# Attention's small products in one run, and their sums moved ahead of the main products

## The chip, the cores and the metric

One core of a Trainium2 chip runs the whole program. The metric is the device time of the program in microseconds; the median of three runs is given, and one further execution was recorded by the profiler.

## The reference

The input x has 4 sequences of 512 times, 128 features and 64 channels (a time holds D = 8192 numbers). Layer 0 is an attention-like recurrence, a convolution over features, a convolution over time and a feed-forward net; layer 1 is a Fourier filter with a moving average. All is fp32. Cut to what matters here:

```python
xn = layernorm(x.reshape(b, t, d), ln_attn_g, ln_attn_b)
k, v, r = xn @ Wk, xn @ Wv, sigmoid(xn @ Wr)          # 64 wide
s = decay * s + k[t] * v[t]                           # over t
x = x + ((r * states) @ Wo).reshape(b, t, f, h)       # 64 -> 8192
xn = layernorm(x.reshape(b, t, d), ln_freq_g, ln_freq_b)
x = x + gelu(conv3_over_f(xn, freq_W) + freq_b)       # mixes the 64 channels
xn = layernorm(x.reshape(b, t, d), ...)               # then causal taps over t,
x = x + layernorm(taps3_over_t(xn))                   # channel by channel
x = x + gelu(x @ ffn_W1 + ffn_b1) @ ffn_W2 + ffn_b2
# layer 1
trend = moving_average(x, 25)
x = trend + irfft(einsum(rfft(x - trend)[:128], w_real + 1j * w_imag))
```

## The kernel before

A tile holds one chunk of D on the 128 partitions and 512 times along the free dimension; two chunks are worked on together, so a stage over one sequence has NPR = 32 steps. Layer 0's stages over a sequence b are generators: `project` (J: the products with Wk, Wv, Wr), `scan` (Z: the recurrence), `attend_and_convolve` (A: the changed one), `convolve_time` (C), `open_feed` (O) and `feed_forward` (F). The function `in_turn` runs two lists of stages side by side, each stage yielding shares of its work, and takes the list that is behind; so A0 (A of sequence 0) runs beside J1, A1 beside C0, A2 beside C1, A3 beside C2. TensorE's order is exactly the order in which the source issues its instructions (`manual_schedule`). On all other engines and on the DMA queues a scheduler orders the instructions.

A step of A works on one pair i of chunks:

- `attend(i)` loads the input pair xp and the weights wo_sb on SP's queue, multiplies the gated state rst with wo_sb into the one PSUM pair a (line 529: two products of 64 rows by 128 columns), adds xp on VectorE into x1 (531) and scales it by the row rb into z (535).
- `convolve(i - 2)` fills a PSUM pair cv. cv is tile c for odd pairs and tile m for even ones, but always c while J1 keeps its own result in m (`held`). Line 550 starts cv with four products that have two rows each: the rows are the convolution's image of the layer norm's scale and bias (`cgr`, loaded once from the DRAM tile `cgd`), times the row mb and a row of ones. Line 559 adds the neighbouring chunks (64x64 products), line 564 the chunks themselves (128x128, "main"). ScalarE applies gelu in place (565), VectorE adds x1 into x2 (567), POOL's queue stores x2 to DRAM (568), ScalarE squares it (570).
- `add_up(i - 3)` adds up x2 and its square over partitions, by products with ones of 32 columns, into the bank st (line 252; convolve_time's own sums go to bank p by the same line).

`x1`, `xp` and `wo_sb` have three buffers, `x2` and its square two. When the sums over all pairs are done, `finish` and `rows` make the mean and the scale of the next layer norm from them and spread them as rows for the next stage. The first stage, `project(0)`, runs alone: for each pair it loads weights, input pair xp and a slab xk in [time, D] order; the weights are multiplied with each other (399), scaled in place on VectorE (358) and used (409), while `statistics` (341) takes mean and variance of the slab on VectorE.

Every fp32 product is two instructions on TensorE, so "x4" in a row is two products.

Of the kernel before, what the change touches and what calls it, by code (L numbers as in the profile page):

```python
# [16 lines left out]
P = 128  # L17
T = 512
NF = 128
H = 64  # L20
# [60 lines left out]
def layer0(ctx, tc, dram, x, xt, vecs, wkvr, wo, wdec, wconv, fbias, w1, fb1, w2, fb2, x4):  # L81
# [67 lines left out]

    cgr = const.tile([P, NPR, H], F32, name="cgr")  # L150

# [17 lines left out]
    def prepare():  # L169
# [35 lines left out]
        for k in range(2):  # L205
            nc.scalar.dma_start(cgd[:, k, :], cgt[k * NCH : (k + 1) * NCH, :])
        cg4 = cgd.rearrange("(i j) k (h m) -> h j k i m", j=2, h=2)
        for h in range(2):
            for j in range(2):
                q = 32 * (2 * h + j)  # L210
                nc.scalar.dma_start(cgr[q : q + 2, :, :], cg4[h, j])

# [112 lines left out]
    def project(b):  # L325
# [41 lines left out]
        for i in range(NPR):  # L367
            first, last = i == 0, i == NPR - 1
            if b > 1:


                xks[i] = token_major(i, two(bk, "sq" if i % 2 else "x2"))
                if i % 2 == 0:
                    weights(i + 2)
                if not last:
                    xps[i + 1] = load_x(b, i + 1)
                wq, xp = ws.pop(i), xps.pop(i)
                for k in (i - 2, NPR - 2, NPR - 1) if last else (i - 2,):
                    if k in xks:
                        statistics(k, xks.pop(k))  # L380
            else:
                if unscanned[0]:

                    wq, xk = two(fr, "x1")[:, :, 0 : 4 * S + 3], spare("z", SL)
                else:

                    both = spare("wx", 4 * S + SL)
                    wq, xk = both[:, :, 0 : 4 * S], both[:, :, 4 * S :]
                n = 4 * S + 2 * (b == 0)
                nc.sync.dma_start(wq[:, :, 0 : n], wkvr[2 * i : 2 * i + 2, :, 0 : n].rearrange("c p s -> p c s"))  # L390
                xp = load_x(b, i)
                statistics(i, token_major(i, xk))
            if b == 0:
# [9 lines left out]
            if b < 2:  # L403
                scale_weights(i, wq)
            elif not last:
                scale_weights(i + 1, ws[i + 1], True)
# [108 lines left out]
    def attend_and_convolve(b):  # L515
# [3 lines left out]
        nc.vector.tensor_scalar(mb, mb, at_one[:, 1:2], at_one[:, 0:1], ALU.mult, ALU.add)  # L519
        x1s, zs, ws, waiting = {}, {}, {}, {}  # L520

        def attend(i):
            xp = load_x(b, i)
            wo_sb = fr.tile([P, P], F32, tag="wo", name="wo_sb")
            nc.sync.dma_start(wo_sb, wo[:, i, :])
            at = two(ps_a, "a")
            for j in range(2):
                js = slice(j * S, (j + 1) * S)
                nc.tensor.matmul(at[:, j, :], lhsT=wo_sb[js, :], rhs=rst[js, :], start=True, stop=True)  # L529
            x1 = x1s[i] = fr.tile([P, 2, SL], F32, tag="x1", name="x1")  # L530
            nc.vector.tensor_tensor(x1, at, xp, ALU.add)  # L531
            z = fr.tile([P, 2, SL], F32, tag="z", name="z", bufs=4)
            for j in range(2):
                zs[2 * i + j] = z[:, j, :]
            nc.vector.tensor_tensor(z, x1, pair_of(rb), ALU.mult)

        def scaled(i):

            wcs = fr.tile([P, 2, P + H], F32, tag="wcs", name="wcs")
            for j in range(2):  # L540
# [3 lines left out]

        def convolve(i):
            cv = c_bank() if i % 2 or held[0] else two(ps_m, "m")
            for h in range(2):
                for j in range(2):
                    q = 32 * (2 * h + j)
                    nc.tensor.matmul(  # L550
                        cv[h * H : (h + 1) * H, j, :], lhsT=cgr[q : q + 2, i, :], rhs=mb[q : q + 2, :],
                        start=True, stop=False,
                    )
            for j in range(2):
                c = 2 * i + j
                for n, h in neighbours(i % 2, c):
                    if 0 <= n < NCH:
                        rs = halves[rows_of(n // 2 % 2, n - c)]
                        nc.tensor.matmul(
                            cv[halves[h], j, :], lhsT=ws[n][rs, P:], rhs=zs[n][rs, :], start=False, stop=False  # L560
                        )
            for j in range(2):
                c = 2 * i + j
                nc.tensor.matmul(cv[:, j, :], lhsT=ws[c][:, 0:P], rhs=zs[c], start=False, stop=True)
            nc.scalar.activation(cv, cv, AF.Gelu_apprx_tanh)
            x2 = two(bk, "x2")
            nc.vector.tensor_tensor(x2, cv, x1s.pop(i), ALU.add)  # L567
            nc.gpsimd.dma_start(x2d[b][2 * i : 2 * i + 2].rearrange("c p t -> p c t"), x2)
            sq2 = bk.tile([P, 2, SL], F32, tag="sq", name="sq2")
            nc.scalar.activation(sq2, x2, AF.Square)  # L570
# [6 lines left out]

        for i in range(NPR + 3):

            while begin[attend_and_convolve] < b + (min(i, 3) - 3) / 4:  # L580
                yield BLOCKED
            if i < 2:
                scaled(i)
            if i < NPR:
                attend(i)
                yield 1.0
            if 1 < i < NPR + 2:
# [7 lines left out]
            if i > 2:  # L595
                add_up(st, i - 3, *waiting.pop(i - 3), i == 3, i == NPR + 2)
                yield 1.0
            if b == 0 and i >= NPR and i < NPR + 2:
# [598 lines left out]
```

## Time and profile before

| | us |
|---|---|
| median of 3 runs (3730.09 to 3739.56) | 3737.65 |
| the profiled execution | 3734.79 |
| its span, first to last instruction | 3733.0 |
| TensorE (PE) busy in it | 3521.2 |
| VectorE (DVE) busy in it | 2671.9 |
| ScalarE (ACT) busy in it | 1778.0 |

PE is TensorE's matmuls, PEld its weight loads (which overlap), DVE VectorE, ACT ScalarE, POOL GpSimd, SP the engine that issues most loads. Where a stretch is asked for, a row gives its bounds, its length, and the busy time of each engine with the number of instructions. In a listing in order of time, the columns are start, length, engine, line, operation, output and inputs, and in brackets the idle time before it with what ended it. Matmul ends are modelled, so the distances of starts say more than lengths. The attentions lie at these times: A0 from 220 to 475 us, A1 from 475 to 802, A2 from 1217 to 1463, A3 from 1873 to 2121; J0 fills 0 to 156, layer 1 everything from 2750 on.

### The profile page before, as it was taken

The numbers are of one execution on the slowest core, as the hardware profiler recorded it, in microseconds if no ns is written. First come the engines' busy times: TensorE is split into PE (matmuls) and PEld (weight loads), VectorE is DVE, ScalarE is ACT, GpSimd is POOL, SyncE is SP. The second block draws the span as 40 slices with busy tenths as digits, with TensorE's granted clock in tenths as the row PEclk, the third lists the DMA queues.
The fourth block names the chain that finished last, engine by engine and source line by source line (L and its number), as shares of the span: only waits on it lengthen the run. The fifth ranks groups of instructions, "written<-read, shape, count | busy, mean of one in ns | idle before, by whom it ended". The sixth has DMA issues, their size and how long they took to land. (4 is left out here: it accounts for less than half of the span.)

```text
span 3733.0 us, 53000 instructions
## 1 busy us (share of the span) xinstructions
PE 3521.2 (94%) x20041; PEld 1360.6 (36%) x20041; DVE 2671.9 (72%) x3498; ACT 1778.0 (48%) x2331; POOL 447.3 (12%) x654
## 2 busy tenths in 40 slices
PE   9999999999998999999989989999989999989998
PEld 4433322234333223433322233333323843328533
DVE  4455569976776896676789699946658277792677
ACT  0012346655656565565656578868854200152100
POOL 0000012210101221001122122100000000001000
PEclk9999999999999999999999999999999999999999
DMA  9867657787874687788578677645569478894687
GB/s 314 279 211 242 227 177 262 260 276 265 290 262 168 235 280 271 266 292 278 182 238 286 213 247 267 234 149 196 198 203 287 150 240 290 290 297 164 213 294 260
DMA packets 427223, 910.29 MB, mean 244 GB/s; under 512 B 32728, under 2 KB 83160, under 8 KB 422872
## 3 DMA queue, kind: packets, MB, share of 16 engines
q1 hardware_dynamic: 353136, 636.92, 52.5%
q0 software_dynamic: 71680, 268.46, 19.7%
q8 instruction: 160, 2.62, 0.3%
q10 hardware_dynamic: 2152, 1.51, 0.1%
q14 instruction: 95, 0.78, 0.1%
HBM read 638.26 MB, written 268.50 MB: 243 GB/s over the span
## 5 line engine op out<-in xcount | busy, mean ns | idle before, releaser
L745 PE MATMUL p<-mid,w_sb 64*64 64x512 f32 x2048 | 554.5, 599 | 20.3 <-DVE wx L758 20.3
L745 PE MATMUL pb<-mid,w_sb 64*64 64x512 f32 x2048 | 536.2, 598 | 0.0
L737 ACT ACTIVATE mid<-c,fb_sb 128x1024 f32<-128x1024 f32 x256 | 284.3, 1111 | 97.2 <-PE c L732 94.8
L737 ACT ACTIVATE mid<-m,fb_sb 128x1024 f32<-128x1024 f32 x256 | 284.6, 1112 | 93.5 <-PE m L732 92.1
L732 PE MATMUL c<-x,w_sb 64*64 64x512 f32 x2016 | 281.2, 611 | 13.2 <-ACT mid L737 6.9
L732 PE MATMUL m<-x,w_sb 64*64 64x512 f32 x2016 | 283.0, 612 | 6.7 <-ACT ob L777 4.9
L745 PEld LDWEIGHTS p<-mid,w_sb 64*64 64x64 f32 x2048 | 155.5, 135 | 294.9 <-issue 262.0
L409 PE MATMUL a<-xp,wx 128*128 128x512 f32 x512 | 242.6, 617 | 9.1 <-DVE wx L358 8.6
L1043 ACT COPY two<-a 128x512 f32<-128x512 f32 x64 | 37.5, 585 | 428.9 <-PE a L1038 428.9
L1066 PE MATMUL b<-xin,avg_sb 128*128 128x512 f32 x512 | 230.8, 593 | 3.3 <-DVE xin L1072 3.3
L1072 DVE TENSOR_TENSOR xin<-b,pm 128x512 f32<-128x512 f32 x256 | 159.1, 683 | 100.2 <-PE b L1069 85.3
L570 ACT ACTIVATE sq<-x 128x1024 f32<-128x1024 f32 x128 | 135.1, 1055 | 181.4 <-DVE x L567 181.3
L625 DVE SCALAR_TENSOR_TENSOR to<-kd,vec,to 128x510 f32<-128x510 f32 (+1 forms) x272 | 197.1, 744 | 9.8 <-ACT to L621 8.7
L700 ACT ACTIVATE kd<-kd,vec 128x512 f32<-128x512 f32 x256 | 192.8, 803 | 3.1 <-DVE kd L692 3.1
L252 PE MATMUL st<-x,ones 128*32 128x512 f32 x512 | 176.8, 603 | 13.1 <-DVE x L567 13.1
L925 DVE COPY xf<-b 128x256 f32<-128x256 f32 x128 | 54.4, 425 | 178.3 <-PE b L1012 169.4
L625 DVE SCALAR_TENSOR_TENSOR z<-x,vec,z 128x511 f32<-128x511 f32 x240 | 175.9, 745 | 5.3 <-ACT z L621 3.0
L531 DVE TENSOR_TENSOR x<-a,xp 128x1024 f32<-128x1024 f32 x128 | 156.1, 1220 | 30.6 <-PE a L529 28.4
L703 DVE TENSOR_TENSOR x<-kd,kx 128x1024 f32<-128x1024 f32 x126 | 154.1, 1223 | 32.8 <-ACT kd L700 32.7
L529 PE MATMUL a<-rst,wo_sb 64*128 64x512 f32 x512 | 147.0, 648 | 27.1 <-DVE x L531 25.1
L758 DVE SCALAR_TENSOR_TENSOR x4t<-p,fb_sb,x 128x512 f32<-128x512 f32 x64 | 47.9, 748 | 172.0 <-PE pb L745 169.6
L692 DVE TENSOR_TENSOR kd<-kd,rm 128x1024 f32<-128x1024 f32 x128 | 155.7, 1220 | 7.8 <-ACT rm L286 6.3
(269 smaller groups left out, 6755.1 us busy)
## 6 DMA issues: line engine op xcount, KB each, us to landing
xp<-in_xt SPq DMA_DIRECT2D x256, 512.0 KB
kh<-to SPq DMA_DIRECT2D x156, 512.0 KB
x<-x POOLq DMA_DIRECT2D x128, 512.0 KB, 4.6
kx<-x SPq DMA_DIRECT2D x128, 512.0 KB
x<-ob POOLq DMA_DIRECT2D x64, 1024.0 KB, 8.0
xin<-x SPq DMA_DIRECT2D x64, 1024.0 KB
out<-xin POOLq DMA_DIRECT2D x64, 1024.0 KB, 6.6
x<-x SPq DMA_DIRECT2D x96, 512.0 KB
```

Source lines behind the costliest of these rows:

```text
L252: nc.tensor.matmul(st[32 * q : 32 * q + 32, :], lhsT=ones, rhs=src[:, j, :], start=first, stop=last,)
L409: nc.tensor.matmul(pa[:, k, :], lhsT=wq[:, j, k * P : (k + 1) * P], rhs=xp[:, j, :], start=first and j == 0, stop=last and j == 1,)
L531: nc.vector.tensor_tensor(x1, at, xp, ALU.add)
L625: tap = nc.vector.scalar_tensor_tensor(to[:, j, k:], xr[:, j, : SL - k], vec[:, w, c], to[:, j, k:], ALU.mult, ALU.add)
L692: nc.vector.tensor_tensor(d, d, pair_of(mb), ALU.subtract)
L700: tc.keep_in_program_order(nc.scalar.activation(d[:, j, :], d[:, j, :], AF.Identity, bias=vec[:, B4, c], scale=vec[:, G4, c]))
L703: nc.vector.tensor_tensor(x3, d, x2, ALU.add)
L732: nc.tensor.matmul(pm[halves[j], h, :], lhsT=w1_sb[halves[h], q * H : (q + 1) * H], rhs=x3[halves[h], j, :], start=True, stop=True,)
L737: nc.scalar.activation(mid, pm, AF.Gelu_apprx_tanh, bias=fb1_sb[:, q : q + 1])
L745: nc.tensor.matmul(sums2[i][j][halves[h], :], lhsT=w2_sb[halves[j], q, :], rhs=mid[halves[j], h, :], start=q == 0, stop=q == 3,)
L1066: nc.tensor.matmul(po[j], lhsT=avg_sb[:, j, :], rhs=xin[:, j, :], start=True, stop=False)
L1072: nc.vector.tensor_tensor(by_n(xin[:, j, :]), by_n(po[j]), by_c(pm[j % 2][:, j // 2, :]), ALU.add)
```

## The change

Four things are edited.

1. `attend` cuts its two 64x128 products into four of 64x64.
2. `convolve` is split: a new `around(i)` issues the starting products and the neighbours, `convolve(i)` keeps the main products and what follows. The starting products become 64x64 too: their weights lie in one of three zeroed 128x128 tiles (`cgs`), in which two DMAs per pair, issued on SP two steps ahead in `scaled`, fill the two rows that count in each half.
3. The step's order on TensorE becomes attend, around, sums, main products. For b > 0 the sums lag a further step (`late` = 4), and every third pair of x2 and its square lives in one tile of the tag "ob", which is otherwise feed_forward's output tile. The stage yields once per step, with weight 7.0: for b > 0 ahead of the sums from step 4 on, otherwise at the step's end.
4. In `project` for b < 2, `statistics` is issued after the scaling of the weights.

```diff
-    cgr = const.tile([P, NPR, H], F32, name="cgr")
+    cgs = [const.tile([P, P], F32, name=f"cg{k}") for k in range(3)]
+    for cg in cgs:
+        nc.gpsimd.memset(cg, 0.0)
...
-        cg4 = cgd.rearrange("(i j) k (h m) -> h j k i m", j=2, h=2)
-        for h in range(2):
-            for j in range(2):
-                q = 32 * (2 * h + j)
-                nc.scalar.dma_start(cgr[q : q + 2, :, :], cg4[h, j])
...
-                statistics(i, token_major(i, xk))
+                token_major(i, xk)
...
                 scale_weights(i, wq)
+                statistics(i, xk)
...
             for j in range(2):
-                js = slice(j * S, (j + 1) * S)
-                nc.tensor.matmul(at[:, j, :], lhsT=wo_sb[js, :], rhs=rst[js, :], start=True, stop=True)
+                for hs in halves:
+                    nc.tensor.matmul(
+                        at[hs, j, :], lhsT=wo_sb[halves[j], hs], rhs=rst[halves[j], :], start=True, stop=True
+                    )
...
         def scaled(i):
 
+            for j in range(2):
+                at = H * (j ^ i % 2)
+                nc.sync.dma_start(cgs[i % 3][at : at + 2, :], cgd[2 * i + j])
...
-        def convolve(i):
-            cv = c_bank() if i % 2 or held[0] else two(ps_m, "m")
-            for h in range(2):
-                for j in range(2):
-                    q = 32 * (2 * h + j)
+        def around(i):
+            cv = cvs[i] = c_bank() if i % 2 or held[0] else two(ps_m, "m")
+            for j in range(2):
+                rs = halves[j ^ i % 2]
+                for hs in halves:
                     nc.tensor.matmul(
-                        cv[h * H : (h + 1) * H, j, :], lhsT=cgr[q : q + 2, i, :], rhs=mb[q : q + 2, :],
-                        start=True, stop=False,
+                        cv[hs, j, :], lhsT=cgs[i % 3][rs, hs], rhs=mb[rs, :], start=True, stop=False
                     )
...
+        def convolve(i):
+            cv = cvs.pop(i)
...
-            x2 = two(bk, "x2")
+            if b and i % 3 == 2:
+                both = bk.tile([P, NT, SL], F32, tag="ob", name="both")
+                x2, sq2 = both[:, 0:2, :], both[:, 2:4, :]
+            else:
+                x2, sq2 = two(bk, "x2"), two(bk, "sq")
...
-            sq2 = bk.tile([P, 2, SL], F32, tag="sq", name="sq2")
...
-        for i in range(NPR + 3):
+        late = 4 if b else 3
+        for i in range(NPR + late):
...
             if i < NPR:
                 attend(i)
-                yield 1.0
             if 1 < i < NPR + 2:
-                convolve(i - 2)
-                yield 5.0
...
+                around(i - 2)
+            if b and i > 3:
+                yield 7.0
+            if i >= late:
+                add_up(st, i - late, *waiting.pop(i - late), i == late, i == NPR + late - 1)
+            if 1 < i < NPR + 2:
+                convolve(i - 2)
+            if not b or i <= 3:
+                yield 7.0
```

More of the change, by code (lines that the diff above doesn't have):

```diff
@@ L519, in attend_and_convolve @@
         nc.vector.tensor_scalar(mb, mb, at_one[:, 1:2], at_one[:, 0:1], ALU.mult, ALU.add)
-        x1s, zs, ws, waiting = {}, {}, {}, {}
+        x1s, zs, ws, cvs, waiting = {}, {}, {}, {}, {}
         def attend(i):
@@ L576, in convolve @@
             waiting[i] = x2, sq2
-        for i in range(NPR + 3):
+        late = 4 if b else 3
+        for i in range(NPR + late):
             while begin[attend_and_convolve] < b + (min(i, 3) - 3) / 4:
                 yield BLOCKED
[L582 to L585, printed above, removed]
-                yield 1.0
-            if 1 < i < NPR + 2:
-                convolve(i - 2)
-                yield 5.0
             while i == 3 and feeding[0]:
@@ L594, in attend_and_convolve @@
                 free_s[0] = False
-            if i > 2:
-                add_up(st, i - 3, *waiting.pop(i - 3), i == 3, i == NPR + 2)
-                yield 1.0
+            if i < 2:
+                scaled(i)
+            if i < NPR:
+                attend(i)
+            if 1 < i < NPR + 2:
[4 more added lines that the diff above has]
+                add_up(st, i - late, *waiting.pop(i - late), i == late, i == NPR + late - 1)
+            if 1 < i < NPR + 2:
+                convolve(i - 2)
+            if not b or i <= 3:
+                yield 7.0
             if b == 0 and i >= NPR and i < NPR + 2:
```

## The prediction

> **What bounds the kernel now.** I read the page's busy line first, then cut the span into the stages in which the changed code runs and asked for the busy time of each engine there, then looked at one step in order of time.
>
> ```profile
> PE 3521.2 (94%) x20041; PEld 1360.6 (36%) x20041; DVE 2671.9 (72%) x3498; ACT 1778.0 (48%) x2331; POOL 447.3 (12%) x654
> ```
>
> TensorE is busy 94% of the span, so on the whole time on TensorE is time of the kernel. The changed code runs in four attentions, A0 to A3. By stretch (us; then busy PE, PEld, DVE, ACT, POOL with counts, granted clock, DMA share, GB/s):
>
> ```profile
> 230.00:440.00 210.00, 207.30 (x871) 65.09 (x868) 118.56 (x156) 63.12 (x89) 17.51 (x24) 0.99 0.76 254
> 475.00:537.00 62.00, 55.78 (x305) 18.38 (x308) 34.06 (x39) 24.29 (x36) 8.50 (x12) 1.00 0.44 149
> 537.00:790.00 253.00, 231.50 (x1172) 54.73 (x1168) 251.20 (x273) 156.85 (x215) 70.70 (x92) 1.00 0.77 262
> 1240.00:1440.00 200.00, 194.00 (x1083) 50.58 (x1085) 186.12 (x189) 126.44 (x173) 43.69 (x63) 1.00 0.81 275
> 1895.00:2100.00 205.00, 197.62 (x1115) 51.59 (x1112) 185.84 (x189) 127.98 (x175) 44.47 (x63) 1.00 0.82 278
> ```
>
> A0 (first row) is bound by TensorE: 207.3 of 210 us. A1 has two parts: five steps before the time convolution C0 joins (475 to 537), and 27 steps beside it (537 to 790), where VectorE is busy 251.2 of 253 us: nothing saved on TensorE counts there. A2 and A3 (last two rows, 27 steps each; the same line's x1 additions count them) have TensorE at 97% and 96%, VectorE close behind at 93% and 91%.
>
> One step of A2, TensorE in order of time (start, length modelled, line, tile rows*columns):
>
> ```profile
> 1361.43 1.13 PE L529 MATMUL a<-rst,wo_sb 64*128 64x512 f32 x4
> 1362.49 1.09 PE L550 MATMUL m<-rm,cgr 2*64 2x512 f32 x8
> 1363.51 1.09 PE L559 MATMUL m<-z,wcs 64*64 64x512 f32 x8
> 1364.53 1.98 PE L564 MATMUL m<-z,wcs 128*128 128x512 f32 x4
> 1366.44 0.62 PE L252 MATMUL st<-x,ones 128*32 128x512 f32 x1
> ...
> 1368.30 1.13 PE L529 MATMUL a<-rst,wo_sb 64*128 64x512 f32 x4
> ```
>
> No idle time is shown. Five tile shapes follow each other. Read starts, not lengths: each of the three small groups is two rounds of products and takes 1.06, 1.02 and 1.02 us, together 3.10. And a stretch of the feed-forward, where all products are 64*64:
>
> ```profile
> 2204.07 1.09 PE L732 MATMUL m<-x,w_sb 64*64 64x512 f32 x8 [0.50 <-ACT ob L777]
> 2204.98 0.60 PE L745 MATMUL p<-mid,w_sb 64*64 64x512 f32 x2
> ...
> 2205.41 0.59 PE L745 MATMUL p<-mid,w_sb 64*64 64x512 f32 x2
> ...
> 2205.84 1.04 PE L732 MATMUL c<-x,w_sb 64*64 64x512 f32 x8
> 2206.70 0.60 PE L745 MATMUL p<-mid,w_sb 64*64 64x512 f32 x2
> ...
> 2208.85 0.60 PE L745 MATMUL p<-mid,w_sb 64*64 64x512 f32 x2
> ...
> 2209.39 0.62 PE L252 MATMUL a<-z,ones 128*32 128x512 f32 x1
> ```
>
> Without a change of shape a round starts every 0.43 us (2204.98, 2205.41, 2205.84), also when weights, moving tile and bank change; the first two rounds of a run take 0.91, the last round before another shape 0.54.
>
> [...] 0.54 against 0.43, so about 0.1 us per change. [...] the trace's own DMAs on POOL's queue land in 4.6 us at 512 KB (median), and none of two rows is timed to its landing here.
>
> **The change, part by part.**
>
> *One run of 64x64 products.* Per step, 1.06 + 1.02 + 1.02 = 3.10 us becomes one run of six rounds: 0.91 + 3 x 0.43 + 0.54 = 2.74. Saved: 0.36 us a step. The number of rounds stays (attention's weights are cut in two, but four products run at once instead of two). Sums and main products change places and keep their shapes, so they cost what they did.
> - A0: 32 steps x 0.36 = 11.5. In the built order of the changed kernel, A0 has about seven fewer shape changes more, because the projection's products no longer fall on both sides of the sums: 0.6. Against it: A0 has one bank (c) for the convolution, and the first products into it now come one attend after the projection's, instead of after projection, sums and attend. In a full step, main products end some 4.3 us (8 projection rounds at 0.43, two of attend) before the bank is needed; gelu (1.0) and the x2 addition (1.22) need 2.3. The 2 us of room covers most steps; I charge 3 us in all. Net -9.
> - A1: the first five steps, -1.8. The 27 beside C0: 0 (VectorE hides it). In the built order the row broadcasts that open C0 stand some two steps earlier against A1's. Between 475 and 537 VectorE idles 28 of 62 us; two steps (11 us) of it filled save up to 5. I take -4, between 0 and -9.
> - A2, A3: a step is 200/27 = 7.41 us with 7.19 of TensorE and 6.89 of VectorE; in A3 7.59, 7.32 and 6.88. Less 0.36, TensorE is at 6.83 in A2, below VectorE: the bound passes to VectorE. [...] I keep two thirds: 64 x 0.36 x 2/3 = -15.4, between -6 and -23.
>
> *Sums one step later, third pair.* With late = 4 the sums wait for a square that was made a step before, so that TensorE's waits for x2 and its square (30 and 26 us of weight-load waiting in 537 to 790) go; there VectorE is bound, so it is worth nothing. The wait list of the built order has ACT's square into the third pair wait only for the store of its former use, six steps back. One more step at the end of A1 to A3 holds sums alone: +1 in all.
>
> *Weights by DMA.* Two DMAs of two rows per step, 256 in all, on SP in place of four on ACT, once, for all steps. SP issues a wo_sb load in 0.35 us and ACT one of the old small ones in 0.23, so SP gets 59 to 90 us more over 1000. SP spends 166 of 210 us (550 to 760) and 145 of 210 in A0 waiting for buffers, so this is hidden. Each waits for the products of three steps before, as wo_sb's buffer also does, and lies beside wo_sb in SP's order: xp, wx and x2 loads queue behind it, with three buffers (two for wx) of lead. 256 KB move in all[...]. Cost 0; if the lead were gone, a load late by 1 us in each A0 step costs 32. Three memsets on POOL before 2 us: 0.
>
> *Statistics after the scaling.* The source puts VectorE's statistics later, but the built order has them earlier at the start: statistics of the first slab, the copies of set-up, then only the scaling that TensorE waits for. Before:
>
> ```profile
> 6.07 0.32 DVE L358 TENSOR_SCALAR x<-x,vec 128x192 f32<-128x192 f32 x1 [6.07 <-PE psum_w L399]
> 7.12 4.46 PE L409 MATMUL a<-xp,x 128*128 128x512 f32 x8 [0.23 <-DMA xp<-in_xt]
> 9.09 1.29 DVE L341 BATCH_NORM_STATS2 stt<-z 128x6 f32<-128x512 f32 x2 [1.84 <-DMA z<-in_x]
> ```
>
> The slab lands at 9.09; statistics (1.29) and set-up end at 11.36; the first half of the scaling follows, the second only after half the next slab's statistics (landed 13.96), at 14.9. The first products end near 16.7 instead of 11.4. The projection then runs at TensorE's pace (4.55 us a step), so nothing wins it back: +5, between 0 and +7.
>
> Sum: -9 - 1.8 - 4 - 15.4 + 1 + 5 = -24.2. The profiled execution took 3734.8 us (span 3733.0), so 3710.6; the median of the runs, 3737.65, is 2.9 above it, so about **3713**.
>
> **Rivals.**
> 1. *VectorE takes most of it back.* A2 and A3 give 6 in all, A0 7, A1's early start nothing: -7 - 1.8 - 6 + 1 + 5 = -8.8, 3729 (within what a measurement tells from nothing). For it: 93% of VectorE in A2. Against: in A1 VectorE reaches 99%.
> 2. *The run is no cheaper.* [...] Then only the start's +5 stays: 3742. Against: line L732 to L745 changes all of that at 0.43 us.
> 3. *Slower: A0's one bank.* x2 stands in VectorE's order behind the statistics of the next projection slab, which wait for its load (41.7 us of waits in A0, up to 4.0). If the slab lands more than about 2 us after VectorE asks for it, x2 is late, the bank is late, and all TensorE queued behind the first product into it stands: the sums, main products, projection. About 21 steps carry projection; 3 us each is +63, against -27.2 of all other terms: near 3773. It turns the sign from 1.3 us a step. For it: the room shrinks from 5.4 to 4.3 us. Against: TensorE idles under 3 us in A0 now.
>
> **How the numbers follow.** 0.3% is 11 us, about what a measurement of this kernel can tell from no change. Forecast 0.60 (3695 to 3724, all faster); rival 1 0.18 (two fifths faster, the rest within); rival 2 0.08 (within); rival 3 0.14 (nearly all slower). Faster 0.67, same 0.19, slower 0.14. The range 3690 to 3744 reaches from A2 and A3 keeping all, with A1's full gain (-46, 3692), to rivals 1 and 2; beyond it lie most of rival 3 and a little below.
>
> **What would show it.** The step of A2 in order of time: one 64*64 run of 24 instructions, 2.7 us from its first start to the sums' (3.1 to 3.2 if rival 2). VectorE's busy share in A2 and A3 rises to 95 to 97%, and the stages end 5 to 11 us sooner each; A0's 32 steps 9 us. The first L409-line products end near 16.7 us. Wrong if TensorE waits in A0 before the first product into c for x2 (rival 3), if the DMA of cg is named as a releaser, or if A1's VectorE share falls below 97%.

## The result, and the profile after

The changed kernel took 3754.62 us (median of 4 runs, 3752.58 to 3756.87) against 3736.85 us before; the ratio is 1.0050 (95% interval 1.0033 to 1.0068). Timed once more on another chip it was 3756.18 against 3739.03, ratio 1.0047 (1.0032 to 1.0061). It is **slower by 0.5%, 17 to 18 us**, where 3713 was forecast, outside the range 3690 to 3744.

The profiled execution took 3756.87 us (span 3755.1). Its busy line:

```profile
PE 3473.9 (93%) x20553; PEld 1381.1 (37%) x20553; DVE 2675.7 (71%) x3498; ACT 1778.4 (47%) x2331; POOL 461.6 (12%) x657
```

TensorE is busy 47 us less than before (3521.2) and the span is 22 us longer. The work did become cheaper; the saved time is idle time now, and more besides. By stretch (A0, A1 before C0, A1 beside C0, A2, A3; columns as before, A2's and A3's windows moved with the stages):

```profile
230.00:440.00 210.00, 200.63 (x957) 67.72 (x959) 121.37 (x161) 61.71 (x84) 16.80 (x23) 0.99 0.76 259
475.00:537.00 62.00, 55.75 (x312) 18.11 (x304) 29.94 (x31) 23.21 (x34) 6.42 (x9) 0.97 0.40 132
537.00:790.00 253.00, 209.65 (x1281) 64.66 (x1283) 247.20 (x271) 151.53 (x205) 77.89 (x90) 0.95 0.74 254
1262.00:1462.00 200.00, 184.58 (x1218) 53.76 (x1211) 181.35 (x182) 124.34 (x170) 43.37 (x61) 0.97 0.81 275
1913.00:2118.00 205.00, 187.06 (x1232) 56.09 (x1232) 182.56 (x187) 126.41 (x173) 46.99 (x63) 0.98 0.81 270
```

Read the last three rows: TensorE fell to 83%, 92% and 91%, but VectorE did not rise (A2 91%, A3 89%; forecast 95 to 97%), and the granted clock is under 1.00 (0.95, 0.97, 0.98). Both engines wait for each other: in A2's and A3's rows TensorE waits 15.4 and 16.5 us for VectorE's x1 (L531), and VectorE 13.2 and 17.2 us for gelu (L570) of TensorE's main products.

One step of A2 in order of time, TensorE:

```profile
1384.85 1.98 PE L569 MATMUL m<-z,wcs 128*128 128x512 f32 x4
1386.76 1.09 PE L527 MATMUL a<-rst,wo_sb 64*64 64x512 f32 x8
1387.67 1.04 PE L553 MATMUL c<-rm,cg 64*64 64x512 f32 x8
1388.53 1.04 PE L561 MATMUL c<-z,wcs 64*64 64x512 f32 x8
1389.50 1.06 PE L249 MATMUL st<-both,ones 128*32 128x512 f32 x8
1390.49 1.98 PE L569 MATMUL c<-z,wcs 128*128 128x512 f32 x4
```

From the first attention product to the sums it is 1389.50 - 1386.76 = 2.74 us, as forecast to the hundredth. What was saved there is lost elsewhere. The program was cut at points that all kernels have, and each kernel was profiled twice (the two profiles of before, 3733.0 and 3745.5 us long, show how far a stretch scatters). Differences are of the means, in us:

| stretch | before | after | difference | forecast |
|---|---|---|---|---|
| start to the end of J0 (first L180, then L182) | 156.1, 157.0 | 163.9, 162.8 | +6.8 | +5 |
| to the end of A0 (its `finish`, L264, then L261) | 376.3, 382.0 | 373.0, 370.8 | -7.3 | -9 |
| A1 beside C0, to the first feed-forward (L732, then L744) | 288.7, 287.0 | 302.7, 302.6 | +14.8 | -5.8 |
| to the second feed-forward (holds A2) | 665.9, 666.4 | 659.8, 663.8 | -4.4 | A2 and A3 together |
| to the third (holds A3) | 642.2, 643.4 | 641.8, 644.0 | +0.1 | -15.4 |
| to the end of layer 0 | 620.0, 619.0 | 620.3, 621.0 | +1.2 | 0 |
| between the layers, TensorE idle | 9.5, 9.3 | 16.6, 17.4 | +7.6 | 0 |
| layer 1 | 964.3, 971.4 | 967.0, 962.0 | -3.4 | 0 |

The sum is +15.4. Three rows carry it: the start, A1 beside C0, and the step from layer 0 to layer 1. One expected gain is missing: A2 with A3.

**A0's row hides a shift.** Its end is the first product of A0's `finish`, and two steps of A1 changed sides of it: 37 groups of attention products start ahead of it before (A0's 32 and five of A1), 35 in the changed kernel. (In the kernel before, A0 does not end at 475 us, as the times given above have it, but with its last sums at 526.5.) Cut finer, as means of two profiles: from the end of J0 to A0's first main products +5.7, from there to its last main products -1.5, and from those to `finish` -11.4 (24.8 us before, 13.4 after), where the two steps of A1 are gone. So A0 itself saved next to nothing. The two steps stand in the next row now, and the two rows have to be read together: +7.5, where -14.8 was forecast.

**The start.** TensorE, then VectorE, of the changed kernel:

```profile
4.79 1.96 PE L396 MATMUL psum_w<-x 128*66 128x259 f32 x4 [4.79 <-DMA x<-in_wkvr]
11.46 6.69 PE L407 MATMUL a<-xp,x 128*128 128x512 f32 x8 [4.71 <-DVE x L355]
17.99 1.04 PE L396 MATMUL psum_w<-x 128*66 128x259 f32 x4
```

```profile
8.85 1.29 DVE L338 BATCH_NORM_STATS2 stt<-z 128x6 f32<-128x512 f32 x2 [8.85 <-DMA z<-in_x]
...
11.09 0.32 DVE L355 TENSOR_SCALAR x<-x,vec 128x192 f32<-128x192 f32 x1
13.40 0.69 DVE L338 BATCH_NORM_STATS2 stt<-z 128x6 f32<-128x512 f32 x1 [1.99 <-DMA z<-in_x]
14.01 0.30 DVE L355 TENSOR_SCALAR x<-x,vec 128x192 f32<-128x192 f32 x1
```

The two halves of the first scaling stand at 11.09 and 14.01, as the built order said; the second slab begins at 17.99, before at 11.42:

```profile
11.42 1.04 PE L399 MATMUL psum_w<-x 128*66 128x259 f32 x4
```

**A stall in A2.** Both engines:

```profile
1279.03 1.09 PE L527 MATMUL a<-rst,wo_sb 64*64 64x512 f32 x8
...
1280.06 2.35 DVE L628 TENSOR_TENSOR kd<-kd,rm 128x1024 f32<-128x1024 f32 x2
...
1282.33 2.72 DVE L637 SCALAR_TENSOR_TENSOR to<-kd,vec,to 128x511 f32<-128x511 f32 x4
...
1284.98 1.21 DVE L576 TENSOR_TENSOR x<-m,x 128x1024 f32<-128x1024 f32 x1
...
1286.77 1.21 DVE L531 TENSOR_TENSOR x<-a,xp 128x1024 f32<-128x1024 f32 x1
...
1288.04 1.99 PE L527 MATMUL a<-rst,wo_sb 64*64 64x512 f32 x8 [3.29 <-DVE x L531]
```

The attention products end near 1280, but VectorE empties bank a (L531) only at 1286.77: two subtractions (L628), four taps (L637) of the time convolution, an x2 (L576) and a tap stand ahead of it. The next attention products need the same bank, so TensorE idles 3.29 us, and what follows takes 1.99 us instead of 1.09. The window after it says why (busy PE, PEld, DVE, ACT, POOL, then the clock):

```profile
1287.30:1294.10 6.80, 6.06 (x28) 1.50 (x32) 6.80 (x8) 3.68 (x7) 1.98 (x3) 0.50 0.77 257
```

TensorE ran at half clock (0.50) for 6.8 us. TensorE's waits for x1, summed over A2 and then A3:

```profile
PE a L527 <- DVE x L531: 16.9, 8, 3.5
```

```profile
PE a L527 <- DVE x L531: 18.0, 8, 4.3
```

Before:

```profile
PE a L529 <- DVE x L531: 3.3, 4, 1.4
```

```profile
PE a L529 <- DVE x L531: 5.7, 6, 2.1
```

### The profile page after: what moved, and what is told of

It is laid out like the page before. It is cut to its first block, busy times and chain, and to the rows that moved or that the text cites. A ratio compares the mean times of both kernels' runs of the same rounds, so it can differ in the third digit from the quotient of the medians.

```text
span 3755.1 us, 54524 instructions
## 1 busy us (share of the span) xinstructions
PE 3473.9 (93%) x20553; PEld 1381.1 (37%) x20553; DVE 2675.7 (71%) x3498; ACT 1778.4 (47%) x2331; POOL 461.6 (12%) x657
## 5 line engine op out<-in xcount | busy, mean ns | idle before, releaser
L744 PE MATMUL c<-x,w_sb 64*64 64x512 f32 x2016 | 281.5, 611 | 13.1 <-ACT ob L784 6.6
L744 PE MATMUL m<-x,w_sb 64*64 64x512 f32 x2016 | 282.9, 613 | 6.7 <-ACT ob L789 4.8
L527 PE MATMUL a<-rst,wo_sb 64*64 64x512 f32 x1024 | 147.8, 642 | 79.9 <-DVE x L531 78.3
L637 DVE SCALAR_TENSOR_TENSOR to<-kd,vec,to 128x510 f32<-128x510 f32 (+1 forms) x272 | 195.1, 743 | 4.2 <-issue 1.2
L637 DVE SCALAR_TENSOR_TENSOR z<-x,vec,z 128x511 f32<-128x511 f32 x240 | 175.8, 744 | 5.7 <-ACT z L633 3.6
L531 DVE TENSOR_TENSOR x<-a,xp 128x1024 f32<-128x1024 f32 x128 | 156.1, 1219 | 23.0 <-PE a L527 19.3
L703 DVE TENSOR_TENSOR kd<-kh,rm 128x1024 f32<-128x1024 f32 x128 | 155.6, 1219 | 6.0 <-ACT rm L283 3.2
L535 DVE TENSOR_TENSOR z<-x,rm 128x1024 f32<-128x1024 f32 x128 | 156.3, 1221 | 2.8
```

What stands on the lines that cost most here:

```text
L637: tap = nc.vector.scalar_tensor_tensor(to[:, j, k:], xr[:, j, : SL - k], vec[:, w, c], to[:, j, k:], ALU.mult, ALU.add)
L703: nc.vector.tensor_tensor(d, to, pair_of(rb), ALU.mult)
L744: nc.tensor.matmul(pm[halves[j], h, :], lhsT=w1_sb[halves[h], q * H : (q + 1) * H], rhs=x3[halves[h], j, :], start=True, stop=True,)
```

## The experiments

The loss is made of parts of 3 to 15, and executions of one kernel scatter by some 10 us, so the kernels were timed many times, and are compared by their ratio to the kernel before on the same chip.

**1. The memsets.** In the changed kernel, three memsets of the cg tiles stand ahead of the memsets of the weight tiles in GpSimd's list. Here they are moved behind the first projection; the statistics stay behind the scaling in the source.

```diff
-    for cg in cgs:
-        nc.gpsimd.memset(cg, 0.0)
...
         for _ in project(0):
             pass
+        for cg in cgs:
+            nc.gpsimd.memset(cg, 0.0)
         prepare()
```

> The changed kernel, with the three memsets of the cg tiles emitted after the first projection instead of ahead of it; nothing else moves in the source. Theory S (the memsets stand on GpSimd ahead of the small memsets that the first weight products wait for, and for that alone the planner put VectorE's statistics and set-up ahead of the scaling): with the scaling first again, the first eight products of line L407's form end near 11.5 us instead of 18.0 (second psum product), the first projection ends 6.5 to 8 us sooner (152 to 153.5 instead of 160.0), and the whole is 6 to 8 us shorter, about 3747. Rival S2 (the source's move of the statistics behind the scaling does it, as the prediction took for granted): start unchanged, 3754. Rival S3: the start comes back but later waits absorb it, 3752 or more.

Measured: 3749.53 us, ratio 1.0020 (1.0010 to 1.0030). VectorE scales first again, and TensorE begins the second slab at 12.28:

```profile
7.02 5.43 PE L405 MATMUL a<-xp,x 128*128 128x512 f32 x8 [0.20 <-DMA xp<-in_xt]
12.28 1.04 PE L394 MATMUL psum_w<-x 128*66 128x259 f32 x4
```

In all kernels of this study the second slab began at 17.5 to 18.3 us where the memsets were early, and at 11.1 to 14.0 where they were late. Theory S holds for the cause, and rival S2 is out: the statistics are still behind the scaling here. J0 ended at 160.8, only some 2.5 us sooner than in the changed kernel (163.9 and 162.8): its 17th slab began at 81.5 us (before 80.4), and the second half lost the rest, as rival S3 has it. In the other kernels with late memsets J0 ended at 153.8 to 160.8, with early ones at 160.7 to 163.9. By the ratios this kernel is some 10 us faster than the changed one; what lies beyond J0's 2.5 was not located.

**2. Order and yields of before.** In the attentions only the 64x64 forms, the cg tiles and their DMAs are left of the change.

```diff
-            if b and i % 3 == 2:
...
+            x2, sq2 = two(bk, "x2"), two(bk, "sq")
...
             if i < NPR:
                 attend(i)
+                yield 1.0
             if 1 < i < NPR + 2:
                 around(i - 2)
-            if b and i > 3:
-                yield 7.0
+                convolve(i - 2)
+                yield 5.0
             if i >= late:
                 add_up(...)
-            if 1 < i < NPR + 2:
-                convolve(i - 2)
-            if not b or i <= 3:
-                yield 7.0
+                yield 1.0
...
-        late = 4 if b else 3
+        late = 3
```

> The changed kernel with the order and the yields of the kernel before (attention's products, yield 1, products around and main products together, yield 5, sums one step after, yield 1; no third pair); what stays of the change are the 64x64 forms of attention's and the broadcast products, the cg tiles and their DMAs. Theory L (the single yield hands VectorE and TensorE the partner's work in whole-step lumps; VectorE's order then has x1 behind four taps and two subtractions of the time convolution, the next attention product waits for its one bank, and TensorE stands and falls to half clock): waits of line L527 for x1 go back from 16.9 and 18.0 us to under 6 in each of A2 and A3, the step of 16 us at the end of A0 goes, C0 begins as before, A2 and A3 take some 222 to 228 us each; with the later start (+6.5) and the later layer 1 (+5) still there, the whole is about 3722 to 3732. Rival R (the run of 64x64 itself costs: attention's products come out faster than VectorE can empty them): the waits stay and the whole is 3750 or more.

Measured: 3740.83 us, ratio 0.9995 (0.9980 to 1.0009), 9 us above the upper end of what theory L said. A1 beside C0 took 291.8 us (after: 302.7) and L527's waits in A2 went to 3.2 us. So rival R is out. But A2 and A3 gained nothing (231.0 and 235.1 us from first to last main product; before 232.0 and 234.1): theory L was right on the lumps, wrong on what remains without them.

**3. The yield at the end of the step.**

```diff
-            if b and i > 3:
-                yield 7.0
...
-            if not b or i <= 3:
-                yield 7.0
+            yield 7.0
```

> The changed kernel with its one yield of 7 at the end of the step in every attention, instead of between the products around and the sums; order, third pair and the sums' two steps of delay stay. Theory L2 (what is bad in A1 to A3 is where the yield lies: the partner's VectorE work is planned ahead of x2 and the next x1): VectorE's order has the taps spread, x1 no longer behind four of them, L527's waits in A2 and A3 fall from 16.9 and 18.0 to under 8 us each, and A2 and A3 end 5 to 12 us sooner each, less 0.1 us a step because the two groups of sums no longer stand side by side (5 us in all): about 3742 to 3750. A0 and C0's start don't change (A0's yield was at the end already). Rival L3 (main products behind the sums make x2 late, wherever the yield is): waits and time stay, 3754 to 3759.

Measured: 3748.01 us, ratio 1.0021 (1.0013 to 1.0030), against 1.0047 to 1.0050 for the changed kernel. Where the yield lies costs some 10 us. The waits in A2, then A3:

```profile
PE a L527 <- DVE x L531: 7.9, 6, 2.4
```

```profile
PE a L527 <- DVE x L531: 11.6, 6, 3.9
```

Down from 16.9 and 18.0; A2's is as forecast, A3's above it. In the built order VectorE's taps now stand singly or in twos between other work; with the yield ahead of the sums four stand in a row ahead of x1.

**4. No third pair.** x2 and its square always from their own two buffers, `late = 3`.

> The changed kernel without the third pair and with the sums one step after in every attention (late = 3). VectorE's and SP's order stay the same but for the names. Theory N (the third pair is worth nothing, as predicted): 3750 to 3757, the last step of sums alone gives back 1 us in all. Rival T (the third pair was needed with this order): sums wait for the square of x2 made in the same step, TensorE idles longer in A2 and A3, 3765 or more. Rival V (the third pair in the output tile hurts, by its wait for the store): 3745 or less.

Measured: 3803.62 us, ratio 1.0162 (1.0146 to 1.0177). Theory N fell, by the largest number of this study: by the ratios, **in this order the third pair and the later sums together are worth 42 to 43 us**; they were not taken away one at a time. The waits in A2:

```profile
PE st L249 <- DVE x L572: 19.8, 10, 4.1
PE st L249 <- ACT sq L574: 6.0, 8, 1.9
```

The sums now stand ahead of the main products of the same step, and wait for the x2 and the square of the pair whose main products ended just one short step ago. All of TensorE waits with them.

**5. The room that cgr left.**

```diff
+    pad = const.tile([P, NPR * H - 3 * P], F32, name="pad")
+    nc.gpsimd.memset(pad[:, 0:2], 0.0)
```

> The changed kernel with one more constant tile of 1664 floats a partition, which nothing reads: it takes up the room that cgr left when the three cg tiles replaced it, so later pools lie where they lay before. Theory P (with less room taken, the first slab of the second layer fell on the place of an output tile whose store is the last of the first layer, and waits for it): the idle time of TensorE between the two layers goes back from about 16.6 us to about 9.5, the load's releaser is line L776's transposes' copy or earlier and not the store of ob, and the whole is 5 to 7 us shorter, about 3748. Rival P2 (the second layer has slack later and gives it back): the gap shrinks, the end does not, 3753 to 3757. Rival P3 (not the place, but the order of the loads): gap stays at 16.6.

Measured: 3751.79 us, ratio 1.0028 (1.0013 to 1.0042). The first product of layer 1 and the wait of the slab's load (SP's queue), changed kernel:

```profile
2778.14 4.54 PE L982 MATMUL a<-v,dftd_sb 128*64 128x512 f32 x10 [16.41 <-DMA xin<-x]
```

```profile
SPq L949 <- DMA x<-ob: 43.6, 3, 22.2
```

and with the unused tile:

```profile
2773.66 3.68 PE L984 MATMUL a<-v,dftd_sb 128*64 128x512 f32 x8 [9.25 <-DVE v L972]
```

```profile
SPq L951 <- PE c L778: 37.7, 1, 37.7
```

Theory P holds: with the old layout the load waits for the last transposes of layer 0, with the new one for the store of the last output tile, and TensorE stands 16.4 us instead of 9.3. Every kernel without the tile had 16.6 to 17.5, every one with it 9.0 to 10.5. By the ratios the whole gained 7 to 8 us, about the gap, but the intervals of the two kernels overlap, and layer 1 alone scatters from 957 to 971 us between profiles: rival P2 (part of it given back) is neither shown nor excluded.

**6 and 7. Old order in A0 and A1, or the changed one everywhere; start and room mended in both.** The mixed kernel takes the loop of experiment 2 where b < 2 and that of experiment 3 (third pair, late = 4) where b >= 2; the other is experiment 3 with the two mends.

> Memsets of the cg tiles after the first projection, the unused tile of 1664 floats, the kernel before's order and yields in A0 and A1, and the changed order (third pair, sums two steps late) with its yield of 7 at the end of the step in A2 and A3. Theory V (A1 beside C0 is bound by VectorE, which must do the same 542 us of work before the first feed-forward starts; what counts is its idle time until then, and A0's and A1's new order adds to it): first feed-forward starts 0 to 4 us after that of the kernel before (821 to 825), A2 and A3 last about 220 and 227 us as in the run with the yield at the end, layers 7 us closer; whole 3718 to 3726, below the kernel before by 15 to 22. Rival V2 (A2 and A3 gained only because they came late, their loads being ahead): A2 and A3 last 230 and 234 us again, whole 3735 to 3742.

> As the mixed kernel (memsets later, unused tile), but with the changed order and the yield at the end of the step in all four attentions. Theory V: A0 ends about 9 us sooner than in the kernel before (end of its last sums near 525), but the first feed-forward starts no sooner, at 826 to 832, since VectorE's idle time until then grows; whole 7 to 9 us above the mixed kernel, 3727 to 3735. Rival (A0's gain comes through once the start is mended): first feed-forward at 821 or before, whole at or below the mixed kernel.

Measured on one chip: mixed 3728.40 us, ratio 0.9964 (0.9948 to 0.9981); changed order everywhere 3735.30, ratio 0.9990 (0.9978 to 1.0002). The mixed kernel is the first that beats the kernel before. First feed-forward at 817.2 and 826.4 us. Busy VectorE until the end of A0, and from there to the first feed-forward: before, changed, changed order everywhere with the mends (a window each, busy time, count, clock, DMA):

```profile
0.00:532.40 532.40, 276.77 (x456) 0.98 0.72 242
532.40:821.10 288.70, 265.74 (x302) 0.99 0.76 261
```

```profile
0.00:536.90 536.90, 270.30 (x450) 0.97 0.71 236
536.90:839.60 302.70, 271.90 (x308) 0.95 0.75 256
```

```profile
0.00:528.10 528.10, 270.07 (x450) 0.98 0.71 240
528.10:826.40 298.30, 271.57 (x308) 0.98 0.76 260
```

The sums are the key: 542.5, 542.2 and 541.6 us. Whatever the order, VectorE does the same 542 us before the first feed-forward (540 to 544 in all 17 profiles), so only its idle time until then moves the start of it. With the changed order everywhere A0's `finish` comes at 528.1, 4 us sooner than before, but VectorE has done 6.7 us less by then: two steps of A1 (x1, z and x2 of 1.22 us each are 3.7 us a step) that stood ahead of it now stand in the stretch where VectorE is the bound.

That is the smaller half of the changed kernel's +14.8. The other is idle time of VectorE in the same stretch: 302.7 - 271.9 = 30.8 us (30.8 in the second profile too) against 288.7 - 265.7 = 23.0 (and 21.1). In its middle VectorE is as full as before (from 600 to 700 us 99.2 us busy, before 99.8). What was added stands at the ends, most of it after A1's last steps: ahead of 804.35 and 807.75 us it waits 2.98 and 2.18 us for gelu of the last main products. Before, it has no such wait in the whole stretch.

**8. The kernel before once more.**

> The kernel before, profiled once more, to see how far the landmarks of one kernel scatter: start of A0's first main product 231.2 us, end of A0 532, first feed-forward 821.1, A2 and A3 232.0 and 234.1 us long, layers 9.5 us apart, second layer 964 us. If these hold within 2 us each, the differences of 4 to 10 us between kernels, stage by stage, can be read from single traces; if not, only those that all traces of a kind share.

Measured: 3747.32 us. A0 ended 6.6 us later than in the first profile (one step of 16.31 us where the first had 10.88), layer 1 took 971.4 us; the other stretches held within 2 us. So only stretches outside A0, J0 and layer 1 can be read from a single trace.

**9 to 11. A0 alone in the changed order; A0 and A1 in the run with fine yields; main products ahead of the sums in A2 and A3.** All are edits of the mixed kernel: `old = b == 1`; `attend`, `around`, yield 1, main products, yield 5, sums, yield 1 where b < 2; `attend`, `around`, main products, sums, yield 7 with late = 3 and no third pair where b >= 2.

> The mixed kernel, with the changed order and its single yield in A0 too; A1 stays in the order before. Theory V (what counts for the first feed-forward is VectorE's idle time until then, and A0 in whole steps lets the scan of the next sequence, A1's first steps, and with them VectorE's work, come later against A0's end): A0's last sums end no more than a few us from the mixed kernel's 525, VectorE has done 3 to 6 us less by then, first feed-forward at 820 to 826 against 817, whole 3730 to 3736. Rival (the products' saving of 9 us in A0 comes through when A1 keeps its order): first feed-forward at 814 or before, whole 3724 or less.

> The mixed kernel, with the 64x64 products of A0 and A1 in one run, but the yields fine: attention, around, yield 1, main products, yield 5, sums a step later, yield 1. If the coarse yield was what spoilt A0 and A1, and the run is good for 0.3 us a step in A0, A0 ends 5 to 9 us sooner than the mixed kernel's, VectorE's work done by then is within 2 us of it, and the first feed-forward starts 0 to 5 us sooner (812 to 817); whole 3722 to 3729. Rival (each run empties into one bank a and one bank c, and VectorE is behind with x1 and x2): A0's waits grow and it ends no sooner, whole 3730 or more.

> The mixed kernel, but A2 and A3 with main products ahead of the sums, the sums one step after (late = 3) and no third pair: attention, around, main products, sums, one yield of 7. Theory M (the run and the place of the yield bring the gain; that the sums stand ahead of the main products, and the third pair that this needs, bring nothing, and the two groups of sums stand side by side again, one change of shape less): A2 and A3 last 214 to 220 and 222 to 229 us, whole 3718 to 3728. Rival T2 (the sums, one step after, wait for the squares as in the run without the third pair): A2 and A3 over 235 us each, whole 3745 or more.

Measured on one chip: 3737.11 (ratio 0.9992, 0.9981 to 1.0003), 3738.26 (1.0002, 0.9989 to 1.0015) and 3738.42 (1.0005, 0.9993 to 1.0017). By the whole time they are not told apart. All three lie above the mixed kernel's ratio, the last two clear of its interval, but they ran on another chip, with a J0 up to 7 us longer, and no one stretch of their profiles holds the difference. For A0 in the changed order the time fits theory V, but its cause does not: VectorE had not done less by A0's `finish` (37 groups of attention products ahead of it, A1's row 291.9 us, as with the old order everywhere; one profile), and A0 itself ended 10 us later. So the shift of A1's two steps, and A1's loss with it, comes with A1's own order. For the fine yields the rival fits (the wait for bank c, L553 for x2, is 8.5 us in A0, against 3.7 to 4.3 with the old order), but the whole is within the scatter: **on the whole time both are inconclusive**. For main products first, rival T2 is out (A2 222.3, A3 233.8 us: that order does not need the third pair), but theory M did not come true either: A3 is no shorter than before, and the whole is 10 us above its range.

**12. The changed kernel once more.**

> The changed kernel once more, timed beside the others on one chip: 3750 to 3757, and landmarks within 3 us of the first profile except in A0, where two profiles of the kernel before lay up to 6.6 us apart.

Measured: 3756.18, ratio 1.0047 (1.0032 to 1.0061); its stretches are in the table above.

**13 to 15. The mixed kernel again, its yield cut in two, and the forms alone.** The second splits A2's and A3's yield: 2 after `around`, 5 after the main products. The third is experiment 2 with the two mends: order, yields and pairs of before in all four attentions.

> The mixed kernel once more (old order in A0 and A1, changed order with the yield at the end in A2 and A3, memsets later, unused tile), timed on one chip beside the next two. If its first 530 us were only lucky in the first profile (A0 ended 8 us sooner than in the run with main products first, whose A0 is the same), A0 ends near 530 to 533 and the whole is 3730 to 3735, ratio 0.997 to 0.999; if not, 3724 to 3730, ratio 0.995 to 0.9965.

> The mixed kernel, but with the yield of A2 and A3 cut in two, 2 after the products around and 5 after the main products. The sums of both sequences can then stand side by side and VectorE's order stays spread. If that saves the extra change of shape, 0.1 us a step, A2 and A3 are 3 us shorter each (216 and 226), whole 2 to 6 us under the mixed kernel; if it brings back some of the lumps (x1 behind taps), A2 and A3 are 220 to 226 and 230 to 234 and the whole is 2 to 8 us above it.

> The kernel before's order, yields and pairs in all four attentions, with memsets later and the unused tile; of the change only the 64x64 forms, the cg tiles and their DMAs are left. Its step in A0 should be 9.28 us as in the mixed kernel's A0 (before 9.64), so 0.36 us come from the forms and not from the run. Theory F (that step's gain is all there is in A0 and A1; in A2 and A3, where the run with the old order took 231 and 235 us, the forms alone bring nothing): A2 and A3 230 to 236 us each, the whole 3734 to 3742, ratio 0.999 to 1.001, 8 to 14 us above the mixed kernel. Rival F2 (the forms bring most of the gain everywhere): A2 and A3 below 226 and 230, whole 3730 or less.

Measured on one chip: 3724.89 (ratio 0.9965, 0.9950 to 0.9981), **3721.16 (0.9956, 0.9941 to 0.9972)** and 3728.94 (0.9970, 0.9961 to 0.9979). The mixed gain is real. The forms alone, with nothing of the attentions' order moved, bring 11 of its 13 us; theory F fell in the whole (11 us gained, not none to 4), and held where it spoke of A2 and A3 (231.7 and 234.0 us). The gain is in A0's row: 367.8 us with the same 37 groups in it, against 376.3 and 382.0 before. The split yield is the fastest kernel of the study, 0.44% under the one before; its interval overlaps those of the other two. A step of A2 of the forms-alone kernel:

```profile
1367.11 1.09 PE L527 MATMUL a<-rst,wo_sb 64*64 64x512 f32 x8
1368.02 1.04 PE L553 MATMUL c<-rm,cg 64*64 64x512 f32 x8
1368.88 1.04 PE L561 MATMUL c<-z,wcs 64*64 64x512 f32 x8
1369.85 1.98 PE L569 MATMUL c<-z,wcs 128*128 128x512 f32 x4
```

1369.85 - 1367.11 = 2.74 us: the run of 64x64 products is there in the old order too. A0 shows what makes it cheaper, because J1's products part the run in some of its steps. Where they do, attention's products take 1.02 us (before 1.06) and the other two groups 1.88 (before 2.03): 0.19 saved. Where the run is whole it is 3.10 to 2.74, as in A2. So, by estimate from these starts, the saving comes mostly from the changes of shape that go, and only a little (0.04 us, attention's products) from the forms themselves.

So the predicted saving needs no more than the forms, and as far as the stretches of one profile show it, it comes through in A0 alone. What sums ahead of main products, `late` = 4, the third pair and a yield at the end add to it in A2 and A3 is not clear of the noise (0.9964, 0.9965 and 0.9956 against 0.9970). A2 and A3 are shorter with them from first to last main product, but from the first feed-forward to the third the mixed kernel took 1304.0 and 1306.9 us and the split one 1299.5, forms alone 1305.3, the kernel before 1308.1 and 1309.8.

## Why the prediction was wrong, by its own steps

- **The run of 64x64 products: right.** 2.74 us against 3.10, 0.36 a step, in A0, A2 and A3; rival 2 (row halves and banks that change inside a run cost as much as a change of shape) is excluded: inside the run the groups start 0.91 and 0.86 us after one another (1386.76, 1387.67, 1388.53), where before each took 1.02 to 1.06. With fewer changes of shape the same six rounds take less time.
- **A0, -9: the number came by luck, the term failed.** The row gave -7.3, but it lost two steps of A1; A0's own 32 steps took 1.5 us less. The cheaper run is there (the common step is 9.08 us, before 9.64), and forms alone bring the 32 steps from 276.4 and 284.1 us to 269.9. In the changed kernel TensorE's waits took it back: for bank c, charged with 3 us, 7.7 and 7.8 us against 2.7 and 1.4; for x2 ahead of the sums 3.0 against 0.3; and 5.8 against 2.0 in the scan, where two hops stand together because a step of A0 now yields once (one step of 16.3 us, 16.4 in the second profile). So rival 3's wait came, but at a tenth of the 63 us it was given.
- **C0's earlier start and A1, -5.8 in all: the step that failed most, with the wrong sign.** It came out at +14.8, half of the miss of some 41 us. The prediction saw in the built order that C0's rows stand two steps earlier against A1's, and took it as VectorE's idle time filled. It is the reverse: two steps of A1 are pushed from ahead of A0's `finish` into the stretch that VectorE bounds, which puts 6 us more of VectorE's work there, and VectorE stands idle 8 to 9 us more in it. The question to ask was not when C0 starts, but how much of the 542 us VectorE has done by then, and how long it will idle afterwards. With A1 in its old order, and A0 in either, the stretch takes 287.0 to 292.0 us in nine profiles; with A1 in the changed order 298.3 to 311.5 in seven.
- **A2 and A3, -15.4: too much by 11.** From feed-forward to feed-forward they gave -4.3. No kernel of this study reached -15.4 there; the best came to -9. The two thirds that the prediction keeps were the author's estimate. "The bound passes to VectorE" did not happen at 95%: the order of VectorE's own list did. The yield between `around` and the sums puts the partner's taps ahead of x1, and bank a, of which there is one, waits (16.9 and 18.0 us), then half clock (0.50 from 1287.30 to 1294.10). With the yield at the end the first to last main products of A2 and A3 take 220.1 and 226.7 us, 11 and 8 less than before, of which the start of those attentions gives back a part.
- **Sums one step later with a third pair, 0 (and +1): wrong as it was put.** It is 0 only as long as the sums stay behind the main products. With the sums ahead it is a condition of the change, worth 42 to 43 us.
- **The start, +5: right in mechanism, wrong in cause.** +6.8. The order of VectorE came from the three memsets on GpSimd, which the prediction priced at 0. They delay nothing on the chip (the first weight tile's memset moves from 1.03 to 2.35 us, and the products that need it wait for a load until 4.8); what they changed is the order that the scheduler built (experiment 1).
- **Not seen: the room.** Taking cgr out moved what lies behind it, and a load of layer 1 fell on the place of layer 0's last output tile: +7.6 between the layers.
- **DMAs of cg on SP, 0: right.** The only waits that name them are two of 0.3 us, of weight loads. That they land in time was the author's estimate: no run times their landing.
- **One sum is off.** "A2 and A3 keeping all, with A1's full gain" gives -9 - 1.8 - 9 - 23 + 1 + 5 = -36.8 by the prediction's own terms. Its -46 needs the start, the extra steps and A0's charge of 3 at 0 as well. The forecast does not rest on it.

What stays open: what A0's changed order alone costs once A1's is the old one (experiments 9 and 10 are within the scatter of A0 and of the chip); why VectorE stands idle longer at the end of A1 in the changed order; why the scheduler answers to the memsets as it does; and how much of the 7 us between the layers reaches the end.

## What to carry to other kernels

Where one engine is saturated in a later stretch, price a change by that engine's ledger: its whole work until the stretch ends is fixed (here 540 to 544 us in 17 profiles), so only its idle time counts, and a stage that ends sooner because it moved that engine's work behind the stretch's start has gained nothing. So check that a stretch holds the same work before and after. When products, yields or buffers move, read the in-order list of the engine that empties the one-bank tile: the instruction that frees the bank must not stand behind a partner's lump. And separate a cheaper form from the reordering that comes with it: here the form alone brought 0.3%, and what came with it took 0.8% away.

## What the runs showed of the hardware

By estimate from these traces, a change of tile shape costs 0.1 to 0.2 us here. A round of 64x64 products starts 0.43 us after the one before, and the last one ahead of another shape takes 0.54. With two changes gone, six rounds went from 3.10 to 2.74 us; with one of them gone, four rounds went from 2.03 to 1.88.

Four 64x64 instructions shared a round in the feed-forward of the kernel before: two into p start at 2204.98 us, two into pb at 2205.00, and the next two into p at 2205.41.

```profile
2205.00 0.59 PE L745 MATMUL pb<-mid,w_sb 64*64 64x512 f32 x2
```

A short wait could cost TensorE twice here. It stood 3.29 us in A2 until 1288.04; its clock was 0.50 from 1287.30 to 1294.10, and a group of two rounds took 1.99 us instead of 1.09. In the scan's hop in A0 it stood 5.82 us until 472.48, and the clock was half from 468.1 to 478.3. In the clock records of the two profiles such stretches lasted 3.41, 6.83 or 10.24 us within the layers; the changed kernel's profile has 41 of all kinds, that of before 26. In A2 the mean clock was 0.97 with the yield ahead of the sums, and 1.00 with the yield at the end. Here the length of a wait alone does not tell whether one follows: in the changed kernel waits of 2.41 us before 785.0 and 2.66 before 1966.7 were followed by a stretch of 3.41 us, while two of 2.95 and 3.00 us in A3 (before 1991.7 and 2053.0) were followed by none (clock 1.00). By estimate from the case in A2: at half clock TensorE lost half of the 6.06 us from 1288.04 to 1294.10, so its wait of 3.3 us cost some 6.
